# Value products per 256 queries, row sums divided out on leaving PSUM, and separate buffers for position copies

One core of a Trainium2 chip (trn2) runs a kernel of two attention layers. The metric is the time of one execution on the device, in microseconds. Engines are named PE (TensorE), DVE (VectorE), ACT (ScalarE), POOL (GpSimd) and SP (the queue that issues most DMAs).

## The reference

Input: four images of 32 x 32 positions and 768 channels. Each of two layers is group norm, attention with 12 heads of 64 channels and a bias from relative positions, an output projection and a residual. The two layers differ only in scale, biases and the size of the position tables.

```python
x = x + attention(group_norm(x))            # two layers
# attention, per image and head, S = 1024 positions, d = 64:
scores = scale * q @ k.T + rel_h[..., :, None] + rel_w[..., None, :]
attn   = softmax(scores, axis=-1)
out    = (attn @ v).reshape(...) @ Wproj + bproj
```

## The kernel before

The heads go in pairs: 8 image-layers x 6 pairs = 48 pairs. For a pair, each block of 128 queries passes through this chain: PE makes scores in PSUM; POOL has prepared the bias sum in `sc`; DVE adds both and takes the row extreme; ACT makes the exponentials and their row sums; POOL divides; DVE transposes within 32 x 32 squares; a DMA writes the result to DRAM (`td`); another reads it back turned (`pt`); PE multiplies with the values (`av`). Fillers for PE are the projections of the next pair (`pj`) and the output projection (`o`). All but PE is ordered by the framework's scheduler.

```python
scpool = ...(name="sc", bufs=6)   # 4 KB each, for scores, and also for t and v below
tbpool = ...(name="tb", bufs=4);  ptpool = ...(name="pt", bufs=1)

def positions(g, i):              # q times the position tables
    ...
    t = scpool.tile([P, 4, 2, P], FP, tag="sc")          # a buffer of the scores' pool
    nc.scalar.copy(t, ps.rearrange("p h j r -> p j h r"))
    nc.scalar.dma_start(out=td[...], in_=t...)           # tdr <- t, rel is read from it

def biases(g, n):
    for h in range(2):
        sc = scpool.tile([P, HW, HW], FP, tag="sc")
        nc.gpsimd.tensor_tensor(sc, rel_h..., rel_w..., ALU.add)

def scores(g, n):
    ...                                                  # matmuls, DVE reduction, ACT exp
    nc.vector.reciprocal(st[:, 2, :], st[:, 1, :])
    for h in range(2):
        nc.gpsimd.tensor_scalar(sc, sc, st[:, 2, h : h + 1], 1.0, ALU.mult, ALU.mult)

def turn(g, n):
    for h in range(2):
        nc.vector.transpose(tb[:, :, j, :], sc_of[g, n, h])
        if j == 1:                                       # every second block
            nc.sync.dma_start(out=td, in_=tb...)         # 8 KB per partition
            nc.sync.dma_start(out=pt[:, quarter]..., in_=td...)      # pieces of 2 KB

def weigh(g, half):                                      # 512 queries at a time
    for k in range(NT):
        for h in range(2):
            nc.tensor.matmul(av[rows, :], lhsT=v_of[g][:, k, rows], rhs=pt_of[g, half, h]..., ...)
    ...                                                  # DVE copies av to attn
```

## Time and profile before

| | before |
|---|---|
| median time | 4025.5 us |
| PE busy | 95% |
| DVE, POOL busy | 58%, 57% |
| DMA queue of SP, share of 16 engines | 73.6% |
| granted TensorE clock | 0.980 |

In a line of groups come source line, engine, operation, output and inputs with shapes, count, busy time and mean ns of one; then the idle time before the group and what ended most of it. A matmul in fp32 is two instructions on PE (3072 for the 1536 score products). A line of waits reads "who, at which line, waited for whom: total us, times, longest". A "run" of matmuls below is an unbroken row of the timeline, such as the 12 instructions of one projection. Times "from start to start" count a run to the start of the next one on PE, so all the waiting is inside them.

### The profile page before, as it was taken

The page shows a single profiled execution, that of the slowest core. Times are in us where ns is not written, and L with a number is a line of the kernel's source. Part 1 is how long each engine was busy: PE and PEld are TensorE (multiplying, and loading weights), DVE is VectorE, ACT ScalarE, POOL GpSimd, SP SyncE. Part 2 cuts the span into 40 slices and gives each one's busy share as a digit, 9 for nine tenths or more (in the row PEclk, how much of TensorE's full clock was granted, in tenths as well). Part 3 has the DMA queues.
Part 4 walks back from the last instruction along what each step waited for, and adds up shares of the span by engine and source line. Part 5 has one row for each costly group of instructions (what it writes and reads, how often), then busy time and mean ns, then how long its engine had stood idle before and what let it go on. Part 6 is the DMA issues. An engine that isn't in the chain of part 4 may idle for free.

```text
span 4008.2 us, 39298 instructions
## 1 busy us (share of the span) xinstructions
PE 3795.4 (95%) x13056; PEld 1577.2 (39%) x13056; DVE 2324.9 (58%) x3520; ACT 1150.5 (29%) x1848; POOL 2300.8 (57%) x1555
## 2 busy tenths in 40 slices
PE   7989899999999999999999998999999999999998
PEld 3334333433344334444344343433344343434332
DVE  4555655547565565656665566555665566546653
ACT  2233223322232222322232223323233222322320
POOL 4656556655666546656556565655556565556661
PEclk9999999999999999999999999999999999999998
DMA  4777777878787787877877787878877788778867
GB/s 166 247 260 266 284 257 278 299 248 290 257 288 276 260 300 253 295 268 278 285 275 277 266 298 280 278 251 288 301 264 265 266 287 305 261 248 283 288 250 244
DMA packets 615612, 1084.89 MB, mean 271 GB/s; under 512 B 234481, under 2 KB 295153, under 8 KB 566257
## 3 DMA queue, kind: packets, MB, share of 16 engines
q1 hardware_dynamic: 564720, 1032.05, 73.6%
q10 hardware_dynamic: 50688, 50.34, 3.7%
q8 instruction: 103, 1.69, 0.2%
q14 instruction: 101, 0.82, 0.1%
HBM read 578.92 MB, written 503.32 MB: 270 GB/s over the span
## 4 chain that ended last, share of the span: by engine, by line
PE 61%; DMA 11%; DVE 10%; POOL 6%; ACT 5%; issue 5%; SPq 1%; ACTq 0%; DVEq 0%; POOLq 0%
PE pj L225 20%; PE av L372 17%; PE s L320 11%; PE o L425 9%; DMA tdr<-t 8%; DVE tb L356 4%; ACT sc L331 4%; POOL sc L308 3%; POOL sc L338 3%; DVE sc L327 3%; PE tp L276 3%; DMA pt<-td 2%; DVE st L155 1%; ACT t L281 1%; PE vt L261 1%
## 5 line engine op out<-in xcount | busy, mean ns | idle before, releaser
L308 POOL TENSOR_TENSOR sc<-rel 128x1024 f32<-128x1024 f32 x768 | 1451.6, 1910 | 578.2 <-DMA tdr<-t 341.4
L225 PE MATMUL pj<-xn,w 128*128 128x512 f32 x3456 | 1581.4, 607 | 1.1 <-DVE xn L201 1.1
L331 ACT ACTIVATE sc<-sc,sm 128x1024 f32<-128x1024 f32 x768 | 878.6, 1145 | 2063.0 <-DVE sm L327 1558.6
L338 POOL TENSOR_SCALAR sc<-sc,sm 128x1024 f32<-128x1024 f32 x768 | 849.1, 1118 | 1063.1 <-DVE sm L335 1028.8
L356 DVE STREAM_TRANSPOSE tb<-sc 128x1024 f32<-128x1024 f32 x768 | 917.9, 1226 | 741.5 <-POOL sc L338 740.3
L225 PEld LDWEIGHTS pj<-xn,w 128*128 128x128 f32 x3456 | 640.3, 192 | 924.5 <-issue 908.9
L327 DVE CUSTOM_DVE_ANT_0 sc<-s,sc 128x1024 f32<-128x1024 f32 x768 | 905.8, 1214 | 159.3 <-PE s L320 155.8
L320 PE MATMUL s<-k,q 64*128 64x512 f32 x3072 | 844.7, 623 | 54.3 <-DVE sm L327 54.3
L372 PE MATMUL av<-pt,v 128*64 128x512 f32 x3072 | 706.9, 606 | 34.1 <-DMA pt<-td 10.2
L425 PE MATMUL o<-attn,wo 128*128 128x512 f32 x1152 | 537.6, 615 | 26.3 <-DVE res L432 21.2
L320 PEld LDWEIGHTS s<-k,q 64*128 64x128 f32 x3072 | 294.0, 189 | 461.0 <-issue 288.7
L372 PEld LDWEIGHTS av<-pt,v 128*64 128x64 f32 x3072 | 264.4, 139 | 462.6 <-issue 369.1
L425 PEld LDWEIGHTS o<-attn,wo 128*128 128x128 f32 x1152 | 213.2, 193 | 333.8 <-issue 272.2
L335 DVE RECIPROCAL sm<-sm 128x2 f32<-128x2 f32 x384 | 63.5, 165 | 441.5 <-ACT sc L331 441.5
L379 DVE COPY attn<-av 128x256 f32<-128x256 f32 x192 | 71.9, 416 | 251.1 <-PE av L372 251.0
L281 ACT COPY t<-tp 128x1024 f32<-128x1024 f32 x96 | 97.1, 1012 | 285.4 <-PE tp L276 277.9
L276 PE MATMUL tp<-tab,q 64*128 64x128 f32 x1536 | 111.6, 285 | 42.3 <-ACT q L238 20.9
L331 ACT ACTIVATION_READ_ACCUMULATOR sc<-sc,sm 128x1 f32 x768 | 143.2, 186 | 0.0
L276 PEld LDWEIGHTS tp<-tab,q 64*128 64x128 f32 x1536 | 93.3, 187 | 108.9 <-ACT q L236 40.5
L262 ACT COPY v<-vt 128x512 f32<-128x512 f32 x96 | 55.9, 583 | 219.4 <-PE vt L261 218.4
L261 PE MATMUL vt<-ident,v 128*128 128x128 f32 x384 | 60.0, 280 | 34.1 <-DVE res L432 28.8
L261 PEld LDWEIGHTS vt<-ident,v 128*128 128x128 f32 x384 | 46.1, 142 | 92.5 <-DVE res L432 40.4
(45 smaller groups left out, 655.7 us busy)
## 6 DMA issues: line engine op xcount, KB each, us to landing
td<-tb SPq DMA_DIRECT2D x384, 1024.0 KB, 6.1
pt<-td SPq DMA_DIRECT2D x384, 1024.0 KB, 7.2
w<-in_wqkv SPq DMA_DIRECT2D x144, 384.0 KB, 7.2
tdr<-t ACTq DMA_DIRECT2D x96, 512.0 KB, 7.6
rel<-tdr SPq DMA_DIRECT2D x768, 32.0 KB, 2.0
part<-res SPq DMA_DIRECT2D x96, 256.0 KB, 5.3
res<-part SPq DMA_DIRECT2D x96, 256.0 KB, 5.1
wo<-in_wo SPq DMA_DIRECT2D x84, 192.0 KB, 4.4
```

Of the source, the lines that this page charges most:

```text
L225: nc.tensor.matmul(t, lhsT=w[:, c, :], rhs=xn[c][:, cols], start=(c == 0), stop=(c == NC - 1),)
L261: nc.tensor.transpose(t[:, j, :], qkv_of[g, 2][:, at * P : (at + 1) * P], ident)
L276: nc.tensor.matmul(ps[:, h, j, :], lhsT=q[rows, at * P : (at + 1) * P], rhs=tabs[l][rows, :], start=True, stop=True,)
L281: nc.scalar.copy(t, ps.rearrange("p h j r -> p j h r"))
L308: nc.gpsimd.tensor_tensor(sc, rel[:, h, 0, n, :].unsqueeze(2).to_broadcast([P, HW, HW]), rel[:, h, 1, n, :].unsqueeze(1).to_broadcast([P, ...
L320: nc.tensor.matmul(ps[h][:, cols], lhsT=q[rows, n * P : (n + 1) * P], rhs=k[rows, cols], start=True, stop=True,)
L327: nc.vector.tensor_tensor_reduce(out=sc, in0=ps[h], in1=sc, scale=-1.0, scalar=BIG, op0=ALU.add, op1=ALU.min, accum_out=st[:, 0, h : h + 1],)
L331: nc.scalar.activation(sc, sc, AF.Exp, bias=st[:, 0, h : h + 1], scale=-1.0, accum_out=st[:, 1, h : h + 1],)
L338: nc.gpsimd.tensor_scalar(sc, sc, st[:, 2, h : h + 1], 1.0, ALU.mult, ALU.mult)
L356: nc.vector.transpose(tb[:, :, j, :], sc_of[g, n, h])
L372: nc.tensor.matmul(av[rows, :], lhsT=v_of[g][:, k, rows], rhs=pt_of[g, half, h][:, :, :, k, :].rearrange("p q r t -> p (q r) t"), start=(k ...
L425: nc.tensor.matmul(t, lhsT=w[:, c - c0, :], rhs=attn_of[im * NP + c][:, cols], start=(c == c0), stop=(c == c1 - 1),)
```

## The change

The intent was to take the division from POOL, to make the pieces of work smaller so that the buffers of turned weights can be doubled, and to keep position copies from holding score buffers. The row sums must then divide the products, whose columns are queries. So their reciprocals have to lie along the columns, equal in all 64 rows of a head. The change sends them through DRAM for that: a write (`rd`), then a broadcast read (`rb`). Core of the diff:

```diff
-    scpool = ...(name="sc", bufs=6)      # 6 x 4 KB
-    tbpool = ...(name="tb", bufs=4);  ptpool = ...(name="pt", bufs=1)
+    scpool = ...(name="sc", bufs=3)      # 3 x 8 KB, both heads
+    tmppool = ...(name="tmp", bufs=2)    # position copies t, and v before its turn
+    tbpool = ...(name="tb", bufs=2);  ptpool = ...(name="pt", bufs=2);  rbpool = ...(name="rb", bufs=3)
 ...
-            early.append(lambda: positions(g, i))
+            (later if pair else early).append(lambda: positions(g, i))     # one step later
 ...
-        for h in range(2):
-            nc.gpsimd.tensor_scalar(sc, sc, st[:, 2, h : h + 1], 1.0, ALU.mult, ALU.mult)
 ...
+        nc.vector.transpose(tb..., sc_of[g, n]...)       # both heads, 2048 elements
+        nc.sync.dma_start(out=td[:, j].rearrange("h p s -> p h s"), in_=tb)
+        if j == 1:
+            nc.sync.dma_start(out=pt..., in_=td...)      # 2 MB in pieces of 1 KB
+            nc.vector.reciprocal(st[:, 2]..., st[:, 1]...)
+            rd = dram2.tile([2, 2 * P], FP, tag="rd")
+            nc.sync.dma_start(out=rd.rearrange("h (n p) -> p (h n)", p=P), in_=st[:, 2]...)
+            for h in range(2):
+                nc.sync.dma_start(out=rb[h * D : (h + 1) * D, :], in_=rd[h : h + 1, :].to_broadcast([D, 2 * P]))
 ...
-    def weigh(g, half):                   # 512 queries
+    def weigh(g, quarter):                # 256 queries
 ...
+        nc.vector.tensor_tensor(attn_of[g][:, at : at + 2 * P], av, rb_of[g, quarter], ALU.mult)
```

More of the change, by code (lines that the diff above doesn't have):

```diff
@@ L59, in attention_blocks @@
     vpool = ctx.enter_context(tc.tile_pool(name="v", bufs=2))
-    scpool = ctx.enter_context(tc.tile_pool(name="sc", bufs=6))
-    tbpool = ctx.enter_context(tc.tile_pool(name="tb", bufs=4))
-    ptpool = ctx.enter_context(tc.tile_pool(name="pt", bufs=1))
+    scpool = ctx.enter_context(tc.tile_pool(name="sc", bufs=3))
+    tmppool = ctx.enter_context(tc.tile_pool(name="tmp", bufs=2))
+    tbpool = ctx.enter_context(tc.tile_pool(name="tb", bufs=2))
+    ptpool = ctx.enter_context(tc.tile_pool(name="pt", bufs=2))
+    rbpool = ctx.enter_context(tc.tile_pool(name="rb", bufs=3))
     relpool = ctx.enter_context(tc.tile_pool(name="rel", bufs=2))
@@ L217, in project_in @@
         if i == 0:
-            pool, tag = (scpool, "sc") if which == 2 else (qkpool, "qk"[which])
+            pool, tag = (tmppool, "tmp") if which == 2 else (qkpool, "qk"[which])
             qkv_of[g, which] = pool.tile([P, S], FP, tag=tag, name=f"{'qkv'[which]}_{g}")
@@ L279, in positions @@
                 )
-        t = scpool.tile([P, 4, 2, P], FP, tag="sc", name=f"t_{g}_{i}")
+        t = tmppool.tile([P, 4, 2, P], FP, tag="tmp", name=f"t_{g}_{i}")
         nc.scalar.copy(t, ps.rearrange("p h j r -> p j h r"))
@@ L298, in positions @@
                         nc.sync.dma_start(out=rel_of[g][32 * y : 32 * y + 32, h, ax, :, :], in_=src)
-    sc_of, tb_of, pt_of, attn_of = {}, {}, {}, {}
+    sc_of, st_of, td_of, pt_of, rb_of, attn_of = {}, {}, {}, {}, {}, {}
     def biases(g, n):
         rel = rel_of[g]
+        sc = scpool.tile([P, 2, HW, HW], FP, tag="sc", name=f"sc_{g}_{n}")
+        sc_of[g, n] = sc
         for h in range(2):
-            sc = scpool.tile([P, HW, HW], FP, tag="sc", name=f"sc_{g}_{n}_{h}")
-            sc_of[g, n, h] = sc
             nc.gpsimd.tensor_tensor(
-                sc, rel[:, h, 0, n, :].unsqueeze(2).to_broadcast([P, HW, HW]),
+                sc[:, h], rel[:, h, 0, n, :].unsqueeze(2).to_broadcast([P, HW, HW]),
                 rel[:, h, 1, n, :].unsqueeze(1).to_broadcast([P, HW, HW]), ALU.add,
@@ L323, in scores @@
                 )
-        st = small.tile([P, 3, 2], FP, tag="sm", name=f"sm_{g}_{n}")
+        if n % 2 == 0:
+            st_of[g, n // 2] = small.tile([P, 3, 2, 2], FP, tag="sm", name=f"sm_{g}_{n}")
+        st = st_of[g, n // 2]
         for h in range(2):
-            sc = sc_of[g, n, h].rearrange("p y x -> p (y x)")
+            sc = sc_of[g, n][:, h].rearrange("p y x -> p (y x)")
             nc.vector.tensor_tensor_reduce(
                 out=sc, in0=ps[h], in1=sc, scale=-1.0, scalar=BIG, op0=ALU.add, op1=ALU.min,
-                accum_out=st[:, 0, h : h + 1],
+                accum_out=st[:, 0, h, n % 2 : n % 2 + 1],
@@ L330, in scores @@
             )
             nc.scalar.activation(
-                sc, sc, AF.Exp, bias=st[:, 0, h : h + 1], scale=-1.0,
-                accum_out=st[:, 1, h : h + 1],
-            )
-        nc.vector.reciprocal(st[:, 2, :], st[:, 1, :])
-        for h in range(2):
-            sc = sc_of[g, n, h].rearrange("p y x -> p (y x)")
-            nc.gpsimd.tensor_scalar(sc, sc, st[:, 2, h : h + 1], 1.0, ALU.mult, ALU.mult)
+                sc, sc, AF.Exp, bias=st[:, 0, h, n % 2 : n % 2 + 1], scale=-1.0,
@@ L340, in turn @@
+                accum_out=st[:, 1, h, n % 2 : n % 2 + 1],
+            )
     def turn(g, n):
-        half, quarter, j = n // 4, n // 2 % 2, n % 2
-        for h in range(2):
-            if n % 4 == 0:
-                pt_of[g, half, h] = ptpool.tile(
-                    [P, 2, 4, NT, 2 * HW], FP, tag=f"pt{h}", name=f"pt_{g}_{half}_{h}"
-                )
-            if j == 0:
-                tb_of[h] = tbpool.tile([P, HW, 2, HW], FP, tag="tb", name=f"tb_{g}_{n}_{h}")
-            tb, pt = tb_of[h], pt_of[g, half, h]
-            nc.vector.transpose(tb[:, :, j, :], sc_of[g, n, h])
-            if j == 1:
-                td = dram2.tile([P, S * 2], FP, tag=f"td{h}", name=f"td_{g}_{n}_{h}")
-                nc.sync.dma_start(out=td, in_=tb.rearrange("p k n i -> p (k n i)"))
-                nc.sync.dma_start(
-                    out=pt[:, quarter].rearrange("p r k t -> p r (k t)"),
-                    in_=td.rearrange("(r j) (y t) -> (j y) r t", r=4, y=4),
-                )
@@ L365, in weigh @@
-    def weigh(g, half):
-        if half == 0:
+        quarter, j = divmod(n, 2)
+        tb = tbpool.tile([P, 2, S], FP, tag="tb", name=f"tb_{g}_{n}")
+        nc.vector.transpose(
+            tb.rearrange("p h s -> p (h s)"), sc_of[g, n].rearrange("p h y x -> p (h y x)")
+        )
+        if j == 0:
+            td_of[g, quarter] = dram2.tile([2, 2, P, S], FP, tag="td", name=f"td_{g}_{quarter}")
+        td = td_of[g, quarter]
+        nc.sync.dma_start(out=td[:, j].rearrange("h p s -> p h s"), in_=tb)
@@ new lines, in turn @@
+        if j == 1:
+            pt = ptpool.tile([P, 2, 2, 4, NT, HW], FP, tag="pt", name=f"pt_{g}_{quarter}")
+            pt_of[g, quarter] = pt
+            nc.sync.dma_start(
+                out=pt.rearrange("p h n r k i -> p (h n r) (k i)"),
+                in_=td.rearrange("h n (r j) (y t) -> (j y) (h n r) t", r=4, y=4),
+            )
+            st = st_of[g, quarter]
+            nc.vector.reciprocal(
+                st[:, 2].rearrange("p h n -> p (h n)"), st[:, 1].rearrange("p h n -> p (h n)")
+            )
+            rd = dram2.tile([2, 2 * P], FP, tag="rd", name=f"rd_{g}_{quarter}")
+            nc.sync.dma_start(
+                out=rd.rearrange("h (n p) -> p (h n)", p=P),
+                in_=st[:, 2].rearrange("p h n -> p (h n)"),
+            )
+            rb = rbpool.tile([P, 2 * P], FP, tag="rb", name=f"rb_{g}_{quarter}")
+            rb_of[g, quarter] = rb
+            for h in range(2):
+                nc.sync.dma_start(
+                    out=rb[h * D : (h + 1) * D, :], in_=rd[h : h + 1, :].to_broadcast([D, 2 * P])
+                )
@@ L367, in weigh @@
+    def weigh(g, quarter):
+        if quarter == 0:
             attn_of[g] = apool.tile([P, S], FP, tag="attn", name=f"attn_{g}")
-        av = ps_m.tile([P, HALF], FP, tag="m", name=f"av_{g}_{half}")
+        av = ps_m.tile([P, HALF], FP, tag="m", name=f"av_{g}_{quarter}")[:, : 2 * P]
         for k in range(NT):
@@ L373, in weigh @@
                     av[rows, :], lhsT=v_of[g][:, k, rows],
-                    rhs=pt_of[g, half, h][:, :, :, k, :].rearrange("p q r t -> p (q r) t"),
+                    rhs=pt_of[g, quarter][:, h, :, :, k, :].rearrange("p n r i -> p (n r) i"),
                     start=(k == 0), stop=(k == NT - 1),
                 )
-        for q in range(2):
-            at = half * HALF + q * 2 * P
-            nc.vector.tensor_copy(
-                attn_of[g][:, at : at + 2 * P].rearrange("p (n r i) -> p r n i", n=2, r=4),
-                av[:, q * 2 * P : (q + 1) * 2 * P].rearrange("p (r n i) -> p r n i", n=2, r=4),
-            )
+        at = quarter * 2 * P
+        nc.vector.tensor_tensor(attn_of[g][:, at : at + 2 * P], av, rb_of[g, quarter], ALU.mult)
     parts = [(im, p, o, i) for im in range(NI) for p in range(2) for o in range(NC) for i in range(2)]
@@ L437, in project_out @@
         yield True
-    early, late = [], []
+    early, later, late = [], [], []
     def run(todo):
@@ L506, in attention_blocks @@
             run(early)
+            early, later = later, early
             if at + 1 < len(units):
@@ L514, in attention_blocks @@
             take(todo, -(-left(todo) // (NT - n)))
-            if n % 4 == 1 and at > 4:
-                weigh(*(units[at - 2][0], n // 4 ^ 1))
+            if n % 2 == 1 and at > 2:
+                weigh(units[at - 2][0], units[at - 2][1] // 2)
             run(ready)
-        weigh(NPAIR - 1, 1)
+        weigh(NPAIR - 1, 3)
         run(early)
```

## The prediction

> **What bounds the kernel now.** The page of the kernel before comes first, its busy shares and then its groups. All three engines that matter run over the whole span, but only one is near its end.
>
> ```profile
> PE 3795.4 (95%) x13056; PEld 1577.2 (39%) x13056; DVE 2324.9 (58%) x3520; ACT 1150.5 (29%) x1848; POOL 2300.8 (57%) x1555
> ...
> L308 POOL TENSOR_TENSOR sc<-rel 128x1024 f32<-128x1024 f32 x768 | 1451.6, 1910 | 578.2 <-DMA tdr<-t 341.4
> L338 POOL TENSOR_SCALAR sc<-sc,sm 128x1024 f32<-128x1024 f32 x768 | 849.1, 1118 | 1063.1 <-DVE sm L335 1028.8
> L356 DVE STREAM_TRANSPOSE tb<-sc 128x1024 f32<-128x1024 f32 x768 | 917.9, 1226 | 741.5 <-POOL sc L338 740.3
> L320 PE MATMUL s<-k,q 64*128 64x512 f32 x3072 | 844.7, 623 | 54.3 <-DVE sm L327 54.3
> L372 PE MATMUL av<-pt,v 128*64 128x512 f32 x3072 | 706.9, 606 | 34.1 <-DMA pt<-td 10.2
> ```
>
> TensorE (PE) is busy for 95%, so taking work off GpSimd (POOL) or VectorE (DVE) gains only what PE waits for them. A run of matmuls that stalls inside still counts as busy, so the true wait is larger than the missing 5%. Therefore I read PE's timeline over the whole span, from the start of each run of matmuls to the start of the next. A run that waits for nothing costs the same each time: 5.35 us for the 12 of a projection (pj), 1.91 for the 8 of a block's scores (s), 7.02 for the 32 of value products (av), 5.25 for 12 of the output projection (o), 0.98 for 16 position products (tp), 0.53 for 4 transposes (vt). By the counts that is 288 x 5.35 + 384 x 1.91 + 96 x 7.02 + 96 x 5.25 + 96 x 0.98 + 96 x 0.53 = 3597 us, with about 45 for the norm's small products 3642, with 14 us before the first matmul 3656. The span is 4008, so PE loses about 350 us to waits. By the kind of run before which or in which it is lost (total from start to start less the sum above): s 874 - 733 = 141, pj 1619 - 1541 = 78, o 560 - 504 = 56, av 716 - 674 = 42, norm and vt 33. This is all that the change can win.
>
> Where s loses its 141 us is seen in one pair of heads. The timeline of PE, of POOL and of DVE there (start, duration, operation; in brackets idle time and its releaser):
>
> ```profile
> 2043.13 1.89 PE L320 MATMUL s<-k,q 64*128 64x512 f32 x8
> 2044.95 5.42 PE L225 MATMUL pj<-xn,w 128*128 128x512 f32 x12
> 2050.29 1.99 PE L320 MATMUL s<-k,q 64*128 64x512 f32 x8
> 2052.21 5.42 PE L225 MATMUL pj<-xn,w 128*128 128x512 f32 x12
> 2057.56 1.12 PE L320 MATMUL s<-k,q 64*128 64x512 f32 x2
> 2059.65 1.98 PE L320 MATMUL s<-k,q 64*128 64x512 f32 x6 [0.97 <-DVE sm L327]
> 2061.56 5.42 PE L225 MATMUL pj<-xn,w 128*128 128x512 f32 x12
> 2066.91 3.09 PE L320 MATMUL s<-k,q 64*128 64x512 f32 x8
> ```
>
> ```profile
> 2042.29 1.91 POOL L308 TENSOR_TENSOR sc<-rel 128x1024 f32<-128x1024 f32 x1 [2.56 <-PE vt L261]
> 2052.41 1.91 POOL L308 TENSOR_TENSOR sc<-rel 128x1024 f32<-128x1024 f32 x1 [8.21 <-issue]
> 2054.30 2.21 POOL L338 TENSOR_SCALAR sc<-sc,sm 128x1024 f32<-128x1024 f32 x2
> ```
>
> ```profile
> 2055.45 2.37 DVE L356 STREAM_TRANSPOSE tb<-sc 128x1024 f32<-128x1024 f32 x2 [6.49 <-POOL sc L338]
> 2057.74 0.71 DVE L242 TENSOR_SCALAR k<-pj,bqkv 128x512 f32<-128x512 f32 x1
> 2058.37 1.21 DVE L327 CUSTOM_DVE_ANT_0 sc<-s,sc 128x1024 f32<-128x1024 f32 x1
> ```
>
> The next bias sum (L308) needs a buffer of the score pool that the position copy t holds until its write to DRAM has landed (7.6 us, issue list; in the waits POOL <- tdr<-t is 341 us in 46 waits, once per pair). Behind it in POOL's order stands the division (L338), behind that DVE's transpose, behind that the reduction (L327) that frees the PSUM of scores. So the scores at 2057.56 take 4.0 us in place of 1.91, and those at 2066.91 take 3.0. In the whole timeline 42 score runs are split like this one, with 83 us lost, and 35 lose another 35.
>
> **What the Trainium skill says.** "TensorE: Matmul & The Clock Gate", on the weight load (LDWEIGHTS), gives its time as columns / 1.2 ns, and Part 1 gives the warm issue gap as N / 2.4 + 2.5 ns. "TensorEngine Tiling (Array Packing)", Key Properties, says that tiles work in parallel and that a change of tiling mode drains the array. The trace agrees: 12 pj steps at 0.43 us would be 5.16 and take 5.35, some 0.19 per change; av has two column tiles side by side, 16 steps of 0.43 in 7.02. The shortest steps are those of tp, 8 of two row tiles with two loads of 128 columns each in 0.98 us, 0.12 each. "DMA: Bandwidth & Descriptors", Specifications, puts full rate at 512 B and up, with read-modify-write below. The trace has no writes of 4 bytes, so it neither agrees nor disagrees there.
>
> **The change, part by part.**
> Value products per 256 queries: 6144 matmuls of half the width in 192 runs. An estimate of a step is 0.43 / 2 plus the page's floor, 0.216 us, in which two loads of 64 columns (2 x 53 ns by the page) fit; tp's 0.12 with larger loads says that the load does not bind. A run is 16 x 0.216 + 0.14 = 3.59, all 192 are 690 against 674: **+16 us** on PE.
> The division leaves POOL: 768 x 1118 ns, and the step exp - reciprocal - POOL - transpose becomes exp - transpose, about 2.8 us shorter. POOL falls to 1450 us, DVE loses 192 copies of 416 ns for as many products of about that length. Transposes are 384 of 2048 elements; 2 x 1067 + 160 = 2.29 us (an estimate from the 1226 of one), 60 us less. None of this was PE time itself.
> Own buffers for t and v (the tmp pool): the 341 us of POOL waits should go, and with them most of the s loss; I take 75% of 141: **-105**. Stretches at image boundaries, where DVE is full with statistics, remain.
> Position products one step later for five pairs of six: PE now waits about 0.8 us for ACT's q in 45 places, 48 us in all (36 to 40 in direct waits on q); five sixths: **-40**.
> A DVE that is not held by POOL empties PSUM of o sooner (vt waits on DVE res 28.8 us by the waits): half of o and vt, **-30**, and of the rest of pj **-10**.
> Transfers: td and pt bytes stay, but pt comes in 393,216 pieces of 1 KB in place of 196,608 of 2 KB, td in 98,304 of 4 KB in place of half as many. New are 98,304 writes of 4 bytes (row sums, 512 per block of 256) and 24,576 reads of 1 KB. The cost of pieces from the queues:
>
> ```profile
> q1 hardware_dynamic: 564720, 1032.05, 73.6%
> q10 hardware_dynamic: 50688, 50.34, 3.7%
> ```
>
> q10 is nearly all 1 KB pieces: 0.037 x 16 x 4008 us / 50688 = 47 ns. In the windows 2053 to 2060, with only rel's 128 B pieces, a mean share of 0.40 at 63 GB/s gives 13 ns. So about 8 ns per extra piece: pt +101 us of 16 engines, td +25, rb +72, row sums +80 at 13 ns each and perhaps +320. From 3110 us (77.6%) to 3390 - 3630, 88 to 94% of the new span. Not the bound on average, but nearer; I allow **+25**.
> Sum: -105 - 40 - 30 - 10 + 16 + 25 = -144, from 4026 to 3882, say **3880 us**.
>
> **The rivals.**
> *The DMA queue takes POOL's place.* The one SP queue waits in order: write, landing (6.1 us), read of 2 MB, then row sums, their landing, broadcast; the 16 rel issues (7.7 us) and their wait for tdr (411 us) stand in the same queue, and tb has half its former memory. For it: the share of 90%, slow 4-byte writes. Against it: a block has two more steps (some 20 us) until its products, as before, where av waited only 10.2 us for pt. If it holds: 3980 - 4100.
> *Weight loads bind the short products.* 6144 loads at the profile's 139 ns would be 854 us against 690: +160, about 4000. The mean is latency, and tp speaks against it.
> *All waits for DVE go.* Then s, tp, o and pj give nearly all: about 3790.
>
> **Range and chances.** The floor is 3656 + 16 and what surrounds the span (18): 3690, not reached with start, norms and image ends. Full success is about 3790; DMA trouble eats what is gained, to about 4000. Eight in ten: 3790 to 4000. Faster by over 2% is below 3945: 0.75; within 2%: 0.17; slower: 0.08.
>
> **What would show it.** Right: POOL <- tdr gone, score runs unsplit at 1.91 us, tp without its 0.8 us, av runs at 3.6, DMA near 90%. Wrong: av runs above 4 us (loads), av or DVE's product waiting for pt or rb, DVE waiting for td (SP queue), a DMA share at 97% or more.

## The result and the profile after

The changed kernel is correct and takes 4934.25 us (4 runs, 4921.82 to 4945.25). The ratio to the kernel before is 1.225 (95% interval 1.221 to 1.229), so it is 22.5% slower. A ratio here is the mean time of one kernel's fast runs over that of the other's in the same rounds, so not quite the quotient of the medians.

The page of the changed kernel, first its engines, then the chain that ended last, then the groups that answer to those of before:

```profile
PE 3918.8 (80%) x16128; PEld 1857.2 (38%) x16128; DVE 2267.6 (46%) x2944; ACT 1151.8 (23%) x1848; POOL 1457.0 (30%) x787
...
DMA 62%; PE 21%; SPq 7%; DVE 5%; issue 4%; ACT 1%; POOL 0%; DVEq 0%; ACTq 0%
DMA td<-tb 27%; DMA pt<-td 17%; DMA rd<-sm 9%; PE av L387 7%; PE pj L228 6%; PE s L323 5%; DMA part<-res 4%; SPq L376 3%; PE o L436 2%; SPq L301 2%; DMA out<-res 2%; DVE sc L333 1%; DVE tb L350 1%; DMA mid<-res 1%; DMA xn<-in_x 1%
...
L311 POOL TENSOR_TENSOR sc<-rel 128x1024 f32<-128x1024 f32 x768 | 1451.3, 1909 | 3358.4 <-DVE tb L350 1680.2
L350 DVE STREAM_TRANSPOSE tb<-sc 128x2048 f32<-128x2048 f32 x384 | 887.0, 2310 | 1786.1 <-DMA td<-tb 1629.0
...
L387 PE MATMUL av<-pt,v 128*64 128x256 f32 x6144 | 844.2, 436 | 539.9 <-DMA pt<-td 501.2
...
L436 PE MATMUL o<-attn,wo 128*128 128x512 f32 x1152 | 610.1, 684 | 380.6 <-DVE v L245 182.4
```

PE is no longer the bound. DMAs make 62% of the chain, and they stand as releasers where POOL stood before: DVE waits 1629 us for block writes to land, PE waits 501 us for the weights' reads. The list of DMA issues (KB each, median us from issue to landing) shows what became slow:

```profile
td<-tb SPq DMA_DIRECT2D x384, 1024.0 KB, 10.3
pt<-td SPq DMA_DIRECT2D x192, 2048.0 KB, 11.7
...
rd<-sm SPq DMA_DIRECT2D x192, 2.0 KB, 12.9
```

The smallest transfer, 2 KB of row sums, takes the longest. The block write, of the same 1 MB as before, went from 6.1 to 10.3 us. The windows around one row-sum write, issued at 2569.02 and landed 10.29 us later, tell more. The columns are the window, busy times with counts for five engines, then TensorE clock, the DMA engines' busy share and GB/s:

```profile
2568.00:2570.00 2.00, 2.00 (x22) 1.58 (x19) 0.00 (x0) 0.00 (x0) 2.00 (x2) 1.00 1.05 421
2570.00:2572.00 2.00, 2.00 (x16) 1.17 (x14) 0.42 (x1) 0.56 (x1) 1.23 (x1) 1.00 0.96 285
2572.00:2574.00 2.00, 2.00 (x10) 0.74 (x7) 0.54 (x1) 0.03 (x1) 0.00 (x0) 1.00 0.81 148
2574.00:2576.00 2.00, 2.00 (x6) 0.83 (x5) 1.84 (x4) 1.27 (x3) 0.00 (x0) 1.00 0.77 45
2576.00:2578.00 2.00, 2.00 (x6) 0.88 (x5) 0.85 (x1) 1.11 (x2) 0.00 (x0) 1.00 0.73 49
2578.00:2580.00 2.00, 2.00 (x10) 0.69 (x8) 1.52 (x2) 0.69 (x1) 0.46 (x1) 1.00 0.76 98
```

For some eight microseconds the 16 engines are three quarters busy and move 45 to 148 GB/s in place of 421. A read of 2 MB (`pt`) was issued at 2571.85, as this began, and landed 14.8 us later. (Shares a little above 1 occur in such short windows.) A row-sum write is issued 192 times. The timelines of DVE and PE some 20 us earlier show how such a late landing reaches PE:

```profile
2547.99 2.31 DVE L350 STREAM_TRANSPOSE tb<-sc 128x2048 f32<-128x2048 f32 x1 [15.48 <-DMA td<-tb]
2550.23 1.09 DVE L245 TENSOR_SCALAR v<-pj,bqkv 128x512 f32<-128x512 f32 x1
```

```profile
2535.74 3.67 PE L387 MATMUL av<-pt,v 128*64 128x256 f32 x32 [2.34 <-DMA pt<-td]
2539.34 1.99 PE L323 MATMUL s<-k,q 64*128 64x512 f32 x8
2551.37 7.52 PE L436 MATMUL o<-attn,wo 128*128 128x512 f32 x12 [10.04 <-DVE v L245]
```

DVE stands for 15.5 us until a buffer's write has landed. Behind the transpose in its order is the emptying of PSUM (`v`), and PE waits 10 us for that. The run after the wait also takes 7.52 us, not 5.42, and its window shows why: the granted clock (third number from the end) is half.

```profile
2551.00:2553.00 2.00, 1.63 (x2) 0.84 (x3) 2.00 (x5) 0.26 (x1) 2.00 (x2) 0.50 1.38 65
```

The Trainium skill, "TensorE: Matmul & The Clock Gate", Part 1, says that an idle window of about 3.4 us drops the clock to one half; the trace agrees, with 10 us of idle time and a clock of 0.50 behind it, though no run here tests the 3.4 us themselves. The mean granted clock fell from 0.980 to 0.907.

### The profile page after: what moved, and what is told of

Same layout as the page of the kernel before. It is cut to its first block, busy times and chain, and to the rows that moved or that the text cites.

```text
span 4920.1 us, 44373 instructions
## 1 busy us (share of the span) xinstructions
PE 3918.8 (80%) x16128; PEld 1857.2 (38%) x16128; DVE 2267.6 (46%) x2944; ACT 1151.8 (23%) x1848; POOL 1457.0 (30%) x787
## 4 chain that ended last, share of the span: by engine, by line
DMA 62%; PE 21%; SPq 7%; DVE 5%; issue 4%; ACT 1%; POOL 0%; DVEq 0%; ACTq 0%
DMA td<-tb 27%; DMA pt<-td 17%; DMA rd<-sm 9%; PE av L387 7%; PE pj L228 6%; PE s L323 5%; DMA part<-res 4%; SPq L376 3%; PE o L436 2%; SPq L301 2%; DMA out<-res 2%; DVE sc L333 1%; DVE tb L350 1%; DMA mid<-res 1%; DMA xn<-in_x 1%
## 5 line engine op out<-in xcount | busy, mean ns | idle before, releaser
L350 DVE STREAM_TRANSPOSE tb<-sc 128x2048 f32<-128x2048 f32 x384 | 887.0, 2310 | 1786.1 <-DMA td<-tb 1629.0
L387 PE MATMUL av<-pt,v 128*64 128x256 f32 x6144 | 844.2, 436 | 539.9 <-DMA pt<-td 501.2
L436 PE MATMUL o<-attn,wo 128*128 128x512 f32 x1152 | 610.1, 684 | 380.6 <-DVE v L245 182.4
L387 PEld LDWEIGHTS av<-pt,v 128*64 128x64 f32 x6144 | 548.6, 158 | 898.8 <-issue 619.5
L323 PE MATMUL s<-k,q 64*128 64x512 f32 x3072 | 766.6, 617 | 0.6 <-DVE sm L333 0.6
L436 PEld LDWEIGHTS o<-attn,wo 128*128 128x128 f32 x1152 | 242.1, 219 | 736.1 <-issue 311.9
L393 DVE TENSOR_TENSOR attn<-av,rb 128x256 f32<-128x256 f32 x192 | 78.7, 410 | 267.9 <-PE av L387 255.0
L445 DVE TENSOR_TENSOR res<-o,res 128x512 f32<-128x512 f32 x96 | 64.7, 674 | 73.1 <-PE o L436 61.0
L158 DVE BATCH_NORM_STATS2 st<-xn 128x6 f32<-128x512 f32 x96 | 60.0, 667 | 72.1 <-DMA xn<-mid 39.6
L443 DVE SCALAR_TENSOR_TENSOR res<-o,bo,res 128x512 f32<-128x512 f32 x96 | 70.0, 729 | 47.4 <-PE o L436 38.2
## 6 DMA issues: line engine op xcount, KB each, us to landing
td<-tb SPq DMA_DIRECT2D x384, 1024.0 KB, 10.3
```

What stands on the lines that cost most here:

```text
L323: nc.tensor.matmul(ps[h][:, cols], lhsT=q[rows, n * P : (n + 1) * P], rhs=k[rows, cols], start=True, stop=True,)
L350: nc.vector.transpose(tb.rearrange("p h s -> p (h s)"), sc_of[g, n].rearrange("p h y x -> p (h y x)"))
L436: nc.tensor.matmul(t, lhsT=w[:, c - c0, :], rhs=attn_of[im * NP + c][:, cols], start=(c == c0), stop=(c == c1 - 1),)
```

## The experiments

14 kernels ran. My main theory was that the row sums' trip through DRAM is the loss. Its rivals were the halved memory for transposed weights, and the reads in pieces of 1 KB. Most edits change one thing in the changed kernel. But the scheduler orders SP and DVE anew for each kernel, so differences of a few tens of microseconds between variants can't be put down to one line with certainty.

**tb4.** Four buffers for transposed weights:

```diff
-    tbpool = ...(name="tb", bufs=2)
+    tbpool = ...(name="tb", bufs=4)
```

> The changed kernel with four buffers for the transposed weights in place of two, so the memory they had before the change; nothing else. Theory A (two buffers make VectorE wait until a write to DRAM has landed, and that is the loss): the wait of the transposes for the write, 1629 us, falls below 200 us, and the time falls from 4934 to 4000 or less. Theory B (the row sums' round trip through DRAM, in 4-byte pieces, holds the one DMA queue): the wait only moves to the value products; the time stays above 4600.

Measured: 4819.17 us. The wait of DVE for the block writes leaves the list of waits, but the time falls by only 115 us:

```profile
L350 DVE STREAM_TRANSPOSE tb<-sc 128x2048 f32<-128x2048 f32 x384 | 887.3, 2311 | 413.7 <-ACT sc L337 412.9
...
L387 PE MATMUL av<-pt,v 128*64 128x256 f32 x6144 | 873.8, 448 | 746.1 <-DMA pt<-td 710.8
```

The wait moved from DVE to PE, whose idle time before the products rose from 540 to 746 us. The rival of the two buffers falls: they decide where the wait shows, far more than how long it is.

**no_rd.** The trip removed, products multiplied by a constant tile (wrong; it passed the comparison all the same, so in this kernel a pass doesn't prove that the division is right):

```diff
-            rd = ...; nc.sync.dma_start(rd <- st)
-            rb = ...; nc.sync.dma_start(rb <- rd), twice
+            rb_of[g, quarter] = rb_const
```

> The changed kernel without the row sums' round trip: the products leave PSUM multiplied by a constant tile, so the result is wrong on purpose. Two buffers for the transposed weights are kept. Theory B (4-byte writes and the queue's wait for them): landing of the block write falls from 10.3 us back to about 6, the time to 3900 - 4050. Theory A (two buffers alone): little changes, above 4600. Theory C (1 KB pieces of the weights' read make the transfers slow): the read of 2 MB still takes over 11 us to land, the time stays above 4500.

Measured: 3796.62 us, ratio to before 0.942.

```profile
td<-tb SPq DMA_DIRECT2D x384, 1024.0 KB, 6.3
pt<-td SPq DMA_DIRECT2D x192, 2048.0 KB, 9.2
```

Block writes land in 6.3 us again, reads of 2 MB in 9.2, PE is 97% busy, and DVE's wait for block writes is 82 us. The trip is the whole loss and more. Pieces of 1 KB are no cause: they are in this run too. By the SP queue's share they cost 0.802 x 16 x 3797 - 0.736 x 16 x 4008 = 1520 us of engine time for 242,688 more packets, 6 ns each.

**before_rd.** The trip alone, added to the kernel before, its result unused. It is written as two writes of 256 pieces per two blocks.

> The kernel before with the round trip of the row sums added and its result unused: 192 x (512 writes of 4 bytes and 128 reads of 1 KB), same queue. Theory B: the landing of the row sums takes 10 us or more here too, the block writes behind it land late, and the time rises by over 5%, to 4250 or more. If the trip costs only through the two buffers (A), it stays under 4100 here, because four buffers stand ahead of it.

Measured: 5270.93 us, ratio 1.309. The row sums' writes land in 12.6 us and block writes in 10.8. The trip costs 1244 us in the kernel before as well, with its four buffers, so it needs nothing else of the change.

**wr_only.** The write (`rd`) put back into no_rd; nobody reads it or waits for it.

> The run without the trip (3797 us), plus the 4-byte writes alone: 192 writes of 512 pieces, nobody waits for them, the result stays wrong on purpose. If the writes themselves hold the 16 DMA engines (some 7 us each, as the windows after the change suggest: 0.8 busy at 26 to 103 GB/s), the block writes and reads still land late and the time is 4500 - 4900. If the loss came from the queue waiting for the writes to land, it stays under 4000.

Measured: 4849.22 us. So of the 1138 us of the trip (4934 - 3797) the writes alone make 1053. Neither the queue's wait for them nor the broadcast read is needed for the loss.

**wr_pad** and **wr_64.** The same writes, with pieces 512 and 64 bytes apart in place of side by side:

```diff
-            rd = dram2.tile([2, 2 * P], FP, tag="rd")
-            nc.sync.dma_start(out=rd.rearrange("h (n p) -> p (h n)", p=P), in_=...)
+            rd = dram2.tile([4 * P, P], FP, tag="rd")        # wr_64: [4 * P, 16]
+            nc.sync.dma_start(out=rd.rearrange("(x p) e -> p x e", p=P)[:, :, 0:1], in_=...)
```

> As the last one, but each 4-byte piece goes to a line of its own, 512 bytes apart. If the cost is that 512 pieces meet in the same 2 KB of DRAM, the landing falls from 13 us to under 5 and the time to below 4000. If each small write costs by itself, landing and time are within 3% of the last one.

> As the two runs of 4-byte writes alone, with the pieces 64 bytes apart (4849 us with them side by side, 3810 with 512 bytes between). If it is sharing a 64-byte line that costs, about 3810 and a landing near 5 us; if a larger line must not be shared, 4300 - 4850 and a landing of 10 us or more.

Measured: 3809.84 and 3807.70 us, so within 13 us of no writes at all. The issues of wr_only and then of wr_64:

```profile
td<-tb SPq DMA_DIRECT2D x384, 1024.0 KB, 11.2
...
rd<-sm SPq DMA_DIRECT2D x192, 2.0 KB, 14.2
```

```profile
td<-tb SPq DMA_DIRECT2D x384, 1024.0 KB, 6.6
...
rd<-sm SPq DMA_DIRECT2D x192, 2.0 KB, 5.0
```

Count, size and queue are the same; only the distance differs, and the landing falls from 14.2 to 5.0 us. The engine time by the SP queue's shares: 0.818 x 16 x 3812 - 0.802 x 16 x 3797 = 1170 us for 98,304 pieces 64 bytes apart, 12 ns each; side by side it is 0.753 x 16 x 4853 - 48,720 = 9750 us, 99 ns each if all the added time is put on them. The other queue, which does the same work in both, goes from 0.039 x 16 x 3797 = 2370 to 0.067 x 16 x 4853 = 5200 us, so transfers that didn't change are slowed as well, and some of the 99 ns will be such slowing within the SP queue. What costs is that the small writes lie side by side in DRAM, 4 bytes from start to start. Where between 4 and 64 bytes it begins, whether it is shared 64-byte lines or the mere 2 KB in which all 512 pieces meet, and whether it matters that neighbouring pieces may be written by different engines, no run tells.

**rb_only.** no_rd plus the broadcast reads, from a constant row.

> The run without the trip, plus the broadcast reads alone (384 reads of 64 x 1 KB from one constant row in DRAM). By the prediction's 47 ns a piece 72 us of 16 engines: 3800 - 3850 us. If the reads of one row by many hold the queue, over 4000.

Measured: 3829.72 us, 33 more than no_rd. The reads are nearly hidden.

**own_later.** The kernel before with own buffers for t and v, and positions one step later: the part of the change that the prediction credited with most of the gain.

> The kernel before with two parts of the change only: own buffers for position copies and values, and position products one step later. The prediction's part that should win: GpSimd's wait for the position copy's landing (341 us) gone, runs of scores unsplit, 3870 - 3900 us. Rival (the wait is only handed on, to the DMA of the positions or to the transposed weights' queue): 3980 or more.

Measured: 3992.69 us, ratio 0.990. POOL's wait for the position copy is gone from its list, score runs take 752 us from start to start (874 before), `pj` 1584 (1619). But the value products take 878 in place of 716:

```profile
L373 PE MATMUL av<-pt,v 128*64 128x512 f32 x3072 | 784.2, 639 | 124.8 <-DMA pt<-td 100.2
```

The 34 us of idle time before them in the kernel before became 125, with further stalls inside the runs. The rival holds for this part alone: most of what the scores won is lost again in waiting for the weights. Why these come late isn't shown. The single buffer of 512 queries is a candidate, but SP waits 432 us for PE to free it here and waited 464 us in the kernel before, while its wait for block writes to land rose from 637 to 724 us. In the change's form, 256 queries with two buffers, the products take 731 in pool_div (the next run, with the division still on POOL) and 718 in no_rd.

**pool_div.** The changed kernel without the trip, division on POOL as before; correct.

> The changed kernel with the division back on GpSimd ahead of the transpose, as before the change, and so no trip; the result is right. If the division's leaving GpSimd was worth nothing beside the rest, 3790 - 3830 us, as without the trip. If the shorter step from exp to transpose carried part of the gain, 3850 - 3950, with VectorE waiting for GpSimd and the value products for the weights.

Measured: 3943.93 us, ratio 0.979 (interval 0.977 to 0.981, so a gain of about 2%). The transposes wait for POOL again:

```profile
L356 DVE STREAM_TRANSPOSE tb<-sc 128x2048 f32<-128x2048 f32 x384 | 887.6, 2312 | 810.7 <-POOL sc L344 790.9
```

From start to start on PE, scores take 792 us (no_rd 730), `pj` 1613 (1584), `o` 573 (549). Taking the division out of the path from exp to transpose was worth 147 us, the larger part of the 231 us by which no_rd is faster than the kernel before.

**f_act.** As pool_div, division on ACT behind the exps.

> The changed kernel without the trip, the division ahead of the transpose on ScalarE (two scaled copies of some 1.1 us per block, behind the exps of the same block) in place of GpSimd. If it was GpSimd's order, with bias sums of 1.9 us ahead of the division, that made VectorE wait 791 us, 3800 - 3870. If any step between exp and transpose costs as much, 3920 - 3960 as on GpSimd.

Measured: 3891.66 us, ratio 0.968. That is between the two branches of the expectation: of the 147 us, 52 go when the division moves from POOL to ACT, and 95 remain with it on ACT. That the 52 come from POOL's order (bias sums ahead of the division) is likely but not shown.

**f_tr.** A mend: DVE turns the reciprocals in one 128x32 transpose, so the write has 16 pieces of 128 bytes, in four transfers; correct.

```diff
+            nc.vector.reciprocal(wide[:, 0:4], st[:, 1]...)
+            nc.vector.transpose(turned, wide)
+            for b in range(4):
+                nc.sync.dma_start(out=rd.rearrange("h (n b i) -> b (h n) i", b=4, i=HW)[b],
+                                  in_=turned[HW * b : HW * b + 4, :])
```

> The changed kernel, right result, with the row sums turned by VectorE (one 128x32 transpose per 256 queries) so that the write has 16 pieces of 128 bytes in four small transfers, then the same broadcast read. If the cost lies in the 512 small pieces packed side by side, 3830 - 3870 us (the 3830 of the broadcast reads alone, and some for four issues and the wait for them). If any write below 512 bytes into a shared line, or the wait of the queue for the trip, holds the engines, over 4000.

**f_tr_tb3.** The same with three `tb` buffers.

> The mended kernel (row sums turned, 128-byte pieces) with three buffers for transposed weights in place of two, nothing else. If the two buffers cost the difference of 3949 to 3830, VectorE's wait for the block write (473 us) falls below 100 us and the time to 3840 - 3870. If the trip itself does (queue waits and its issues), it stays above 3920.

Measured: 3949.18 and 3992.59 us, ratios 0.981 and 0.993. Most of the loss is gone, but f_tr lies between the two branches of its expectation and doesn't reach rb_only. First a wait of f_tr, then one of f_tr_tb3:

```profile
DVE tb L353 <- DMA td<-tb: 473.0, 107, 11.0
```

```profile
DVE attn L397 <- DMA rb<-rd: 102.8, 24, 6.4
```

With a third buffer the wait for block writes falls from 473 to 25 us, yet the time rises; now DVE's products wait for the broadcast (103 us), and PE's for the weights (102 us). So the two buffers aren't the difference of 119 us to rb_only. What is left is the trip itself, its four writes and the wait for them: SP waits some 200 us in both for the row sums to land. The runs don't separate these parts. Why three buffers are 1% slower than two stays open.

**f_pe** and **f_pe2.** No trip: PE spreads the reciprocals with the identity, ACT copies them out of PSUM; correct. In f_pe the spread comes ahead of the products of its 256 queries, in f_pe2 behind them:

```diff
+        for j in range(2):
+            for h in range(2):
+                nc.tensor.matmul(ps[h * D : (h + 1) * D, j * P : (j + 1) * P],
+                                 lhsT=st[:, 2, h, j : j + 1].to_broadcast([P, D]), rhs=ident, ...)
+        nc.scalar.copy(rb, ps)
         nc.vector.tensor_tensor(attn_of[g][:, at : at + 2 * P], av, rb, ALU.mult)
```

> The changed kernel, right result, with no trip: TensorE spreads the row sums over the 64 rows of a head (four products of 128 columns with the identity per 256 queries, 8 matmuls), ScalarE copies them out of PSUM. An estimate from the 0.12 us of a pair of such short matmuls: 4 x 0.12 x 192 = 92 us more on TensorE than the run without the trip: 3870 - 3910. If the extra runs of short matmuls or the wait for ScalarE's copy cost more, over 3950.

> The spread of the row sums on TensorE as before, but behind the value products of its 256 queries in place of ahead of them, so that no product waits for ScalarE's copy out of the same bank. If that wait was the surplus (90 us of waits in the trace, 187 times), 3890 - 3930. If the short matmuls themselves cost it, above 3960.

Measured: 4006.43 us (ratio 0.995) and 3879.03 us (0.964), the latter a little below its range. In f_pe the products waited for ACT's copy, which reads other columns of the same PSUM bank: the spread takes 234 us from start to start with that wait, 106 in f_pe2. The Trainium skill, "PSUM — Partial Sum Buffer", Terms, says that two engines may not use one bank and quadrant at once, and the framework puts a wait there; the trace shows 186 of them, 90 us. PE in f_pe2:

```profile
2011.91 3.67 PE L378 MATMUL av<-pt,v 128*64 128x256 f32 x32
2015.42 0.61 PE L385 MATMUL av<-ident,sm 128*64 128x128 f32 x8
2015.95 1.99 PE L323 MATMUL s<-k,q 64*128 64x512 f32 x8
```

f_pe2 is the fastest correct version: 3.6% below the kernel before, and 1055 us below the changed one. It takes 82 us more than no_rd: 106 for the spread, while the products take 36 less from start to start.

## Why the prediction was wrong

**The step that failed** is the transfers' term: "row sums +80 at 13 ns each and perhaps +320" us of all 16 engines, "I allow +25". The 13 ns came from reads of 128 bytes. For writes of 4 bytes 64 bytes apart it would have been right (12 ns). But these lie side by side, and each costs 99 ns by the same reckoning (9750 / 16 = 609 us of all 16 engines), which includes what they slow. The term of +25 measured +1053 for these writes alone (wr_only against no_rd). The engines' mean share didn't show it, since 88 to 94% was foreseen and about 82% came: in the windows shown the engines were three quarters busy for eight microseconds while little moved, and the other engines then waited. Of the prediction's signs of being wrong, DVE waiting for td came (1629 us) and av waiting for pt (501 us), but not a share of 97%.

**The rival named the cause among others, and not the size.** "The DMA queue takes POOL's place" named the queue's waits in order, tb's halved memory and slow 4-byte writes, and said 3980 to 4100. The writes were the cause, though by their packing and not by their smallness. The memory was only the place of the wait, and the queue's wait for the row sums isn't needed for it (wr_only).

**The bound and the floor held.** "The floor is 3656 + 16" and "Full success is about 3790" meet no_rd at 3797, a kernel that leaves the trip out. A run of products per 256 queries was to cost 3.59 us; in no_rd one that waits for nothing takes 3.60, so weight loads don't bind.

**Own buffers and later positions** were to bring -105 on scores and -40 on tp. In own_later scores brought -122 and `pj`, where the wait before tp is counted, -35. What was missed is that the gain would turn into a wait for the weights, +162 on `av`. In the change's form, with two buffers of 256 queries, that wait is gone (731 in pool_div).

**"None of this was PE time itself"**, said of the division's leaving POOL, holds for the work but was read as worth nothing, and that was wrong: it is worth 147 us (pool_div against no_rd). So no_rd comes near 3790 by a gain of which the larger part had no term in the prediction's sum. The page before showed it, with DVE waiting 740 us for POOL, and I read only the once-per-pair stall out of that.

**Half of o and vt, -30:** in no_rd they take 603 us in place of 622, so -19.

**Readings that were off, with little effect.** The 42 split score runs lost 111 us, not 83 (start to start less 1.91 each), and the first matmul starts at 6 us, not 14. "Some 0.19 per change" mixes two things: in no_rd the 12 matmuls of `o` take 5.35 us when value products follow, and 5.25 when transposes of the same tile shape do, so a change is worth 0.10. And the formula that the prediction quotes gives 0.216 us for 512 columns where the fp32 steps take 0.43, twice that; "the trace agrees" doesn't hold for it, but the estimate started from the measured 0.43.

## What to carry to other kernels

Count the pieces of a small transfer and ask where they land: 2 KB written as 512 neighbouring 4-byte pieces took longer to land here than a read of 2 MB (14.2 against 12.1 us in wr_only), and a busy share with few GB/s in the windows is how it shows. When a wait is removed from one engine, look for the next buffer that the faster engine will find full, and change both together. A vector that lies along the wrong axis can be turned without DRAM: 0.55 us of TensorE per 256 queries was cheaper here, even with TensorE 97% busy, than the mended trip (3879 against 3949 us).

## What the Trainium skill lacked or had wrong

- "DMA: Bandwidth & Descriptors", Specifications, says that transfers below 512 B go by read-modify-write. The runs show that smallness alone was cheap: 4-byte pieces 64 or 512 bytes apart cost 12 to 16 ns each, and 11 to 13 us of the kernel's time for 98,304 of them. Packed side by side they cost 99 ns each by the queue's share, and 1053 us. The page doesn't have this distinction.
- The same page says that stalled writes hold up an engine's other queues, but only of remote transfers between cores ("Back-pressure in remote DMA"). Here packed small writes to DRAM slowed another queue: that queue's engine time went from 2370 to 5200 us for the same bytes.
- "TensorEngine Tiling (Array Packing)", Key Properties, names the drain on a change of mode without a size: here 0.10 us, 5.35 against 5.25 us for the same run of 12 matmuls.
